# A graph layer on one core: the Relu moves from ScalarE to VectorE, and VectorE's register loads get new places

## The chip, the cores and the metric

The kernel runs on one core of one Trainium2 chip. The metric is device time in microseconds (us) of one execution, and lower is better. The engines are named as in the profile: PE is TensorE (PEld its weight loads), DVE is VectorE, ACT is ScalarE, POOL is GpSimd, SP is SyncE, which here only issues DMAs.

## What is computed

One message-passing layer over 12,500 nodes (48 numbers each) and 400,000 edges, sorted by their target `dst`, with 32 attributes per edge and 128 hidden numbers:

```
h = maximum(layernorm(x), 0)
for each edge e:  pre_e = [h[dst_e], h[src_e], attr_e] @ W1 + b1
                  hid_e = relu(pre_e)
                  msg_e = hid_e @ W2 + b2
out = x + segment_sum(msg, dst)
```

## The kernel before

The first stage (`node_tables`, about 95 us) multiplies the normalised nodes with the two node parts of W1. That leaves `tab_a` (for targets) and `tab_b` (for sources), tables in DRAM with one row of 128 numbers per node, and `bt`, the source table once more, transposed, in SBUF: one node is one column of 128 partitions.

The second stage (`windows`) takes the edges in tiles of 128 and in 391 chunks of 8 tiles. The loop over `c` is unrolled and its order is written by hand: what stands first in the program comes first in the queue of its engine. Three chunks are in work at once. For a chunk:

- **prepare** (chunk c): SP fetches 80 rows of `tab_a` (`rhs`), the edge attributes (`lhs`) and the targets (`row`). GpSimd fetches the source rows of most tiles from `tab_b` into `gb` (L402), one indirect DMA a tile. Each fetch is held back until a marked VectorE instruction some seven chunks earlier has run (`mark`, `paced`), so that the fetches are spread over a chunk. VectorE makes two one-hot patterns, `lhs` (L418) and `hot` (L424).
- **columns**: some tiles are not fetched. Their source rows are copied, one column at a time, from `bt` into a tile `gt` (L359), at an address held in a register. VectorE makes 75 columns a chunk in four parts (19, 20, 20, 16) and ScalarE 72 in five (16, 16, 16, 12, 12), as the table `PARTS` says. Ahead of each part a register load (`load`, L324) reads the addresses from SBUF into registers of that engine. In total 446 of the 3125 tiles are made so, at most two a chunk.
- **before, turned** (chunk c - 1): TensorE multiplies the one-hot `lhs` and the attributes with `rhs` into `pre` in PSUM (L436), and for the tiles made by columns it turns `gt` and adds it there (L445).
- **hidden** (chunk c - 1): VectorE adds `gb` to `pre` in place, for the fetched tiles (L460, 896 or 768 numbers per partition), and then ScalarE makes the Relu of all 1024 into `hid` (L463).
- **fold** (chunk c - 2): TensorE sums `hid` over edges of one target, `p_g` (L471), and counts edges (L476).
- **add** (chunk c - 2): VectorE adds `p_g` into a segment of 1024 nodes in SBUF at a register's place (L490).

Twelve chunks make a segment. At its end VectorE clears the next one and copies the overlap (`segment_next`, L506 and L508). In the next two chunks TensorE multiplies the finished one with W2 (`p_f`, L516 and L517), each half behind `turned`, and VectorE adds it to x (L518) ahead of its `hidden`.

VectorE's queue in one round of the loop before is: lhs, load 0, 19 copies, hot, load 1, 20 copies, load 2, 20 copies, (L518), pre add, load 3, segment add, 16 copies. ScalarE's is: copies of parts 4 to 6, Relu, copies of parts 7 and 8, with one of the loads one chunk ahead.

Of the kernel before, what the change touches and what calls it, by code (L numbers as in the profile page):

```python
# [8 lines left out]
F32 = mybir.dt.float32  # L9
I32 = mybir.dt.int32  # L10
AF = mybir.ActivationFunctionType
ALU = mybir.AluOpType
# [4 lines left out]
P = 128  # L17
N, D, DE, HID, E = 12500, 48, 32, 128, 400000
# [4 lines left out]
T = 8  # L23
CE = T * P
NCH = (NT + T - 1) // T
# [20 lines left out]
BF16 = mybir.dt.bfloat16  # L46
# [13 lines left out]
    (False, 75, 16, 76),  # L60
    (False, 91, 16, 92),
    (False, 107, 16, 108),
    (False, 123, 12, 124),
    (False, 135, 12, 136),
)
PART = sum(n for _, _, n, _ in PARTS)
BASE = 148
DVE_PARTS = sum(dve for dve, *_ in PARTS)
BEHIND = len(PARTS) - 2

BT0 = 16512
SEG0 = 130592
SEG_SIZE = 8 * L


SEG, NEXT, SEG2 = 152, 153, 154
PLACE0 = 155
WIDTH = 156
SLOTS = (NCH + 2 + P - 1) // P
MOST = 32  # L80

# [11 lines left out]
def turned_at(c):  # L93

    return ((), (T - 1,), (T // 2 - 1, T - 1))[len(TURNED.get(c, ()))]
# [16 lines left out]
def node_tables(nc, tc, keep, bt, x, ident, w1, b1, tab_a, tab_b, loads, most, check, rest):  # L112
# [6 lines left out]
    with ExitStack() as es:  # L119
# [3 lines left out]
        ps_n = es.enter_context(tc.tile_pool(name="ps_n", bufs=3, space=PSUM))  # L123
# [9 lines left out]
        xs = []  # L133
# [59 lines left out]
        def table(j, wt, tv, dve):  # L193

            r0, rb = slices[j]
            rows = wt.shape[0]
            t = tabs.tile([P, rb, HID], F32, name="tab")
            for g in range(0, rb // 2, 2):
                n = min(2, rb // 2 - g)
                p_n = ps_n.tile([P, 2, 2 * HID], F32, name="p_n")  # L200
                for q in range(n):
                    nc.tensor.matmul(  # L202
                        p_n[:, q, :], hts[j][:rows, g + q, :],
                        wt.rearrange("k a h -> k (a h)"), start=True, stop=True,
                    )
                to = t[:, 2 * g : 2 * (g + n), :].rearrange("p r h -> p (r h)")
                of = p_n[:, :n, :].rearrange("p q h -> p (q h)")
                if dve and g % 4:
                    nc.vector.tensor_copy(to, of)
                else:  # L210
                    nc.scalar.copy(to, of)  # L211
            nc.sync.dma_start(tv[:, r0 : r0 + rb, :], t)

        def turned(j):
# [3 lines left out]
            for g in range(0, rb // 2, 4):  # L218
                n = min(4, rb // 2 - g)
                for k in range(2):  # L220
# [12 lines left out]
                    else:  # L233
                        nc.scalar.copy(to, of)

        for i in range(ns + 3):
            if i < ns:
                centre(i)
            if 0 <= i - 1 < ns:
                scale(i - 1)  # L240
            if 0 <= i - 2 < ns:
                turn(i - 2)
            if i == ns + 1:
                most()
            if i == ns + 2:
                check()
            if 0 <= i - 3 < ns:
                table(i - 3, wb, tb_v, i >= ns)
        for j in range(ns):
            turned(j)  # L250
        for j in range(ns):
            table(j, wa, ta_v, True)
        rest()


def windows(nc, tc, gp, bt, ident, idx, x_t, tab_a, tab_b, dst, edge_t, w1, w2s, b2s, out_t):
# [3 lines left out]
    with ExitStack() as es:  # L260
# [49 lines left out]
        st = {}  # L310
# [55 lines left out]
        def mark(ins, us):  # L366
            marks.append((ins, us))
# [74 lines left out]
        def turned(c):  # L442

            for t, j in zip(turned_at(c), TURNED.get(c, ())):
                nc.tensor.matmul(st[c]["pre"][:, t, :], gts.pop(j), ident, start=False, stop=True)  # L445

        def hidden(c):
            s = st[c]
            n, pre = s["n"], s["pre"]
            two = len(turned_at(c)) == 2  # L450
            half = T // 2
            to = n - len(turned_at(c))

            def added(x):

                if not two:
                    return x[:, :to, :]
                return x.rearrange("p (b t) h -> p b t h", b=2)[:, :, : half - 1, :]

            mark(nc.vector.tensor_add(added(pre), added(pre), added(s["gb"])), 1.0)  # L460
            spans[c], marks[:] = list(marks), []
            h = wp.tile([P, T, HID], F32, name="hid")
            nc.scalar.activation(h[:, :n, :], pre[:, :n, :], AF.Relu)  # L463
            s["h"] = h

        def fold(c):
            s = st[c]
# [56 lines left out]
        with tc.manual_schedule():  # L524
            for c in range(NCH + 2):
                if c < NCH:
                    prepare(c)
                if c >= NCH:
                    load(c, 0)
                    columns(c, 0)  # L530
                for part in range(1, DVE_PARTS - 1):
                    load(c, part)
                    columns(c, part)
                if 0 <= c - 1 < NCH:
                    before(c - 1)
                if 0 <= c - 2 < NCH:
                    fold(c - 2)
                if 0 <= c - 1 < NCH:
                    turned(c - 1)

                g, k = group(c - 2)
                if k == GQ - 3 or c == NCH - 1:
                    segment_load(g)
                if g > 0 and k < L // BLK:
                    segment_sum(g - 1, k, BLK)
                if g > 0 and k == STORE:
                    segment_store(g - 1, L)
                columns(c, DVE_PARTS)
                for part in range(DVE_PARTS + 1, BEHIND):
                    load(c, part)  # L550
                    columns(c, part)
                if 0 <= c - 1 < NCH:
                    hidden(c - 1)
                if DVE_PARTS > 1:
                    load(c, DVE_PARTS - 1)
                for part in range(BEHIND, len(PARTS)):
                    load(c, part)
                    columns(c, part)
                load(c + 1, DVE_PARTS)
                if 0 <= c - 2 < NCH:  # L560
                    add(c - 2)
                    if k == GQ - 1:
                        segment_next(g)
                if DVE_PARTS > 1:
                    columns(c, DVE_PARTS - 1)
                if c == NCH + 1:
                    segment_sum(g, 0, END_L)
                    segment_store(g, END_L)

                if c < PIECES:  # L570
                    s = slice(c * PIECE, (c + 1) * PIECE)
                    nc.sync.dma_start(out_t[:, s], x_t[:, s])
# [126 lines left out]
def tile_gnn_preln(  # L699
# [60 lines left out]
    with tc.tile_pool(name="keep", bufs=1) as keep, tc.tile_pool(  # L760
# [3 lines left out]
        def loads():  # L764

            nc.sync.dma_start(dsts, dst_cols)
            nc.sync.dma_start(b0f, first_f.rearrange("(o c) -> o c", o=1).to_broadcast([P, NCH]))
            nc.sync.dma_start(far, places)
            nc.sync.dma_start(srci[:, :FIRST], src_cols[:, :FIRST])
            nc.sync.dma_start(last, src_last)  # L770
            nc.sync.dma_start(tab_a[NPAD:, :], zrow)

            nc.gpsimd.tensor_scalar_add(b0f, b0f, HALF)
            full = NT // T
            nc.gpsimd.tensor_tensor(
                rel[:, : full * T].rearrange("p (c t) -> p c t", t=T),
                dsts[:, : full * T].rearrange("p (c t) -> p c t", t=T),
                b0f[:, :full].unsqueeze(2).to_broadcast([P, full, T]), op=ALU.subtract,
            )
# [12 lines left out]

            spare = keep.tile([P, D], F32, name="spare")
            nc.gpsimd.indirect_dma_start(
                out=spare, out_offset=None, in_=x[:, :],
                in_offset=bass.IndirectOffsetOnAxis(ap=srci[:, :1], axis=0),
            )

            rows_of = edge_t.rearrange("d e -> (d e)").rearrange("(n h) -> n h", h=HID)
            for rows in (P, P - 1, P // 2):  # L800
                for k in range(3):
                    unused = keep.tile([P, HID], F32, name=f"unused{rows}_{k}")
                    nc.gpsimd.indirect_dma_start(
                        out=unused[:rows], out_offset=None, in_=rows_of,
                        in_offset=bass.IndirectOffsetOnAxis(ap=srci[:rows, :1], axis=0),
                    )

        def rest():

            nc.sync.dma_start(w2s, w2)  # L810
# [106 lines left out]
```

## Time and profile before

| | before |
|---|---|
| time, median of 3 runs | 3684.37 us (3682.39 to 3684.98) |
| the profiled execution | 3680.5 us, its span 3678.7 us |
| granted TensorE clock, mean | 0.766 |
| GB/s moved by DMA, mean | 95 |

The profile comes from one execution. A row of its groups gives line, engine, operation, what is written and read, shape and count, then the total busy time, the mean length of one in ns, and the engine's idle time just before them with what ended it. "issue" is idle time that ends with nothing that the profile shows: the engine's own sequencer had not yet sent the next instruction. A name such as DVEq means that sequencer. A record of VectorE reaches past the start of the next one, so busy time of a group can be less than count times mean.

### The profile page before, as it was taken

The numbers are of one execution on the slowest core, as the hardware profiler recorded it, in microseconds if no ns is written. First come the engines' busy times: TensorE is split into PE (matmuls) and PEld (weight loads), VectorE is DVE, ScalarE is ACT, GpSimd is POOL, SyncE is SP. The second block draws the span as 40 slices with busy tenths as digits, with TensorE's granted clock in tenths as the row PEclk, the third lists the DMA queues.
The fourth block names the chain that finished last, engine by engine and source line by source line (L and its number), as shares of the span: only waits on it lengthen the run. The fifth ranks groups of instructions, "written<-read, shape, count | busy, mean of one in ns | idle before, by whom it ended". The sixth has DMA issues, their size and how long they took to land.

```text
span 3678.7 us, 108360 instructions
## 1 busy us (share of the span) xinstructions
PE 2699.4 (73%) x17087; PEld 2431.6 (66%) x17087; DVE 3079.3 (84%) x30969; ACT 3154.1 (86%) x28402; POOL 2652.6 (72%) x2715
## 2 busy tenths in 40 slices
PE   8677777767777777777777777767777777777776
PEld 5566666667666666666666766766666666666665
DVE  5688888888888888888888888888888888888886
ACT  4698888888888888888889888888888888888886
POOL 6777777777777777777777777777777777777771
PEclk9677777787787787777777777787777778777777
DMA  5533333333333333333333333333333333333331
GB/s 195 164 94 95 93 88 91 95 87 95 92 94 89 91 88 98 92 94 89 91 91 93 94 94 90 88 95 88 96 92 91 90 91 88 99 91 94 91 93 39
DMA packets 190484, 349.56 MB, mean 95 GB/s; under 512 B 64786, under 2 KB 96932, under 8 KB 188484
## 3 DMA queue, kind: packets, MB, share of 16 engines
q0 software_dynamic: 86768, 176.28, 19.1%
q1 hardware_dynamic: 102736, 166.15, 15.0%
q14 instruction: 581, 4.76, 0.4%
q8 instruction: 139, 2.28, 0.3%
q10 hardware_dynamic: 260, 0.10, 0.0%
HBM read 322.79 MB, written 22.07 MB: 94 GB/s over the span
## 4 chain that ended last, share of the span: by engine, by line
DVE 70%; issue 14%; PE 5%; DVEq 3%; POOL 2%; DMA 2%; ACT 1%; POOLq 0%; ACTq 0%
DVE gt L359 44%; DVE pre L460 9%; DVE hot L424 7%; DVE lhs L418 6%; DVEq L324 3%; DVE seg L490 3%; POOL gb L402 2%; PE p_g L471 2%; DMA gb<-tab_b,srci 2%; PE p_f L516 1%; PE p_f L517 1%; DVE seg L506 1%; DVE xseg L518 1%; PE pre L436 1%; ACT hid L463 0%
## 5 line engine op out<-in xcount | busy, mean ns | idle before, releaser
L402 POOL DMA_INDIRECT gb<-tab_b,srci x2679 | 2617.9, 977 | 941.8 <-issue 493.3
L359 ACT COPY gt<-bt 128x1 f32 x27936 | 2746.5, 187 | 113.3 <-issue 69.7
L359 DVE COPY gt<-bt 128x1 f32 x29152 | 1915.4, 144 | 472.3 <-issue 426.3
L471 PE MATMUL p_g<-hot,hid 128*128 128x80 f32 x6250 | 1122.4, 354 | 937.8 <-ACT hid L463 927.9
L471 PEld LDWEIGHTS p_g<-hot,hid 128*128 128x128 f32 x6250 | 1050.6, 262 | 1013.2 <-ACT hid L463 1002.8
L436 PEld LDWEIGHTS pre<-rhs,lhs 112*128 112x128 f32 x6250 | 984.4, 247 | 85.2 <-issue 85.2
L436 PE MATMUL pre<-rhs,lhs 112*128 112x128 f32 x6250 | 1007.2, 330 | 18.2 <-DMA row<-in_dst 18.2
L463 ACT ACTIVATE hid<-pre 128x1024 f32<-128x1024 f32 x391 | 400.1, 1023 | 353.6 <-DVE pre L460 350.8
L460 DVE TENSOR_TENSOR pre<-pre,gb 128x896 f32<-128x896 f32 (+2 forms) x391 | 418.2, 1070 | 1.5
L424 DVE TENSOR_TENSOR hot<-wnum,rel 128x640 f32<-128x640 f32 x391 | 318.1, 813 | 0.0
L418 DVE TENSOR_SCALAR lhs<-row,bw 80x1024 f32<-80x1024 int16 x391 | 292.0, 747 | 10.4 <-DMA row<-in_dst 10.4
L445 PE MATMUL pre<-ident,gt 128*128 128x128 f32 x892 | 276.4, 418 | 0.3
L476 PEld LDWEIGHTS <-ones 128*128 128x128 bf16 x3125 | 247.9, 135 | 0.0
L476 PE MATMUL p_g<-hot,ones 128*128 128x80 bf16 x3125 | 247.5, 242 | 0.0
L445 PEld LDWEIGHTS pre<-ident,gt 128*128 128x128 f32 x892 | 196.7, 280 | 0.9 <-DVE gt L359 0.5
L490 DVE TENSOR_TENSOR seg<-seg,p_g 128x160 f32 x391 | 124.7, 319 | 13.3 <-DVE pre L460 5.2
L516 PE MATMUL p_f<-seg,w2s 128*48 128x512 f32 (+1 forms) x134 | 108.5, 906 | 0.4 <-DVE seg L490 0.4
L517 PE MATMUL p_f<-seg,b2s 1*48 1x512 f32 (+1 forms) x134 | 86.8, 733 | 0.0
L518 DVE TENSOR_TENSOR xseg<-xseg,p_f 48x512 f32<-48x512 f32 (+1 forms) x67 | 44.9, 670 | 47.4 <-PE p_f L517 47.4
L517 PEld LDWEIGHTS p_f<-seg,b2s 1*48 1x48 f32 x134 | 12.9, 141 | 89.4 <-issue 89.4
L506 DVE MEMSET seg<- 128x944 f32 x64 | 54.1, 845 | 9.5 <-issue 0.3
L211 ACT COPY tab<-p_n 128x512 f32<-128x512 f32 x33 | 18.7, 588 | 21.9 <-PE p_n L202 16.9
(66 smaller groups left out, 276.9 us busy)
## 6 DMA issues: line engine op xcount, KB each, us to landing
row<-in_dst SPq DMA_DIRECT2D x390, 160.0 KB
lhs<-in_edge_t SPq DMA_DIRECT2D x390, 128.0 KB
gb<-tab_b,srci POOLq DMA_INDIRECT x2679
rhs<-tab_a SPq DMA_DIRECT2D x391, 40.0 KB
xseg<-in_x_t SPq DMA_DIRECT2D x33, 192.0 KB
out_x<-xseg SPq DMA_DIRECT2D x33, 192.0 KB
tab_b<-tab SPq DMA_DIRECT2D x3, 1280.0 KB
tab_a<-tab SPq DMA_DIRECT2D x3, 1280.0 KB
```

The source lines that it names most:

```text
L359: done = copy(gts[of][:, e : e + 1], bt8[:, bass.ds(at, 4)].bitcast(F32))
L402: fetch = nc.gpsimd.indirect_dma_start(out=gb[:, t, :], out_offset=None, in_=tab_b[:, :], in_offset=bass.IndirectOffsetOnAxis(ap=srci[:, c ...
L418: mark(nc.vector.tensor_scalar(lhs[:W, : n * P], row[:, : n * P], bw[:, c : c + 1], None, op0=ALU.is_equal,), 0.8)
L424: mark(nc.vector.tensor_tensor(hot[:, :n, :], wnum.unsqueeze(1).to_broadcast([P, n, W]), rel[:, c * T : c * T + n].unsqueeze(2).to_broadca ...
L436: nc.tensor.matmul(pre[:, t, :], s["lhs"][:K, t * P : (t + 1) * P], s["rhs"][:K, :], start=True, stop=t not in turned_at(c),)
L445: nc.tensor.matmul(st[c]["pre"][:, t, :], gts.pop(j), ident, start=False, stop=True)
L460: mark(nc.vector.tensor_add(added(pre), added(pre), added(s["gb"])), 1.0)
L463: nc.scalar.activation(h[:, :n, :], pre[:, :n, :], AF.Relu)
L471: nc.tensor.matmul(p_g[:, 0, :], s["h"][:, t, :], s["hot"][:, t, :], start=t == 0, stop=t == n - 1)
L476: nc.tensor.matmul(p_g[:, 1, :], ones, high[:, t, 1::2], start=t == 0, stop=t == n - 1)
L490: mark(nc.vector.tensor_add(to, to, s["p_g"]), 0.25)
L516: nc.tensor.matmul(p_f[:, :n], w2s, seg[:, 0, s], start=True, stop=False)
```

## The change

`hidden` is split. `gathered` adds `pre` and `gb` on VectorE, but into `hid` in SBUF and not back into PSUM. `hidden` then takes the maximum with zero on VectorE, in place, on the fetched tiles, and a second VectorE instruction takes it from PSUM to `hid` for the one or two tiles made by columns. ScalarE has no Relu any more and only copies columns, in five parts of 16, 80 a chunk. With 155 columns a chunk, 389 * 155 // 128 = 471 tiles are made by columns.

VectorE's queue becomes: lhs, load 0, 19 copies, hot, load 1, 20 copies, (L518), gathered, load 2, 20 copies, hidden (one or two maxima), load 3, segment add, 16 copies. All of ScalarE's loads and copies stand at the end of the round. The new maximum is marked with 0.55 for the pacing of fetches.

Nine GpSimd fetches ahead of the tables whose results nobody reads are left out. A function `unused` is called behind the tables: some twenty small operations on VectorE, 24 on ScalarE and 32 on TensorE, whose results nobody reads.

```
 def hidden(c)  (before)
-            mark(nc.vector.tensor_add(added(pre), added(pre), added(s["gb"])), 1.0)
-            spans[c], marks[:] = list(marks), []
-            h = wp.tile([P, T, HID], F32, name="hid")
-            nc.scalar.activation(h[:, :n, :], pre[:, :n, :], AF.Relu)
-            s["h"] = h
+        def gathered(c):
+            s = st[c]
+            s["h"] = h = wp.tile([P, T, HID], F32, name="hid")
+            mark(nc.vector.tensor_add(apart(c, h, False), apart(c, s["pre"], False), apart(c, s["gb"], False)), 1.0)
+            spans[c], marks[:] = list(marks), []
+
+        def hidden(c):
+            s = st[c]
+            of = apart(c, s["h"], False)
+            mark(nc.vector.tensor_scalar(of, of, 0.0, None, op0=ALU.max), 0.55)
+            if turned_at(c):
+                nc.vector.tensor_scalar(
+                    apart(c, s["h"], True), apart(c, s["pre"], True), 0.0, None, op0=ALU.max
+                )
```

`apart(c, x, by_cols)` gives the tiles of x that were made by columns, or the others. The loop:

```
-                for part in range(1, DVE_PARTS - 1):
-                    load(c, part)
-                    columns(c, part)
+                load(c, 1)
+                columns(c, 1)
...
-                columns(c, DVE_PARTS)
-                for part in range(DVE_PARTS + 1, BEHIND):
-                    load(c, part)
-                    columns(c, part)
+                if 0 <= c - 1 < NCH:
+                    gathered(c - 1)
+                load(c, 2)
+                columns(c, 2)
                 if 0 <= c - 1 < NCH:
                     hidden(c - 1)
-                if DVE_PARTS > 1:
-                    load(c, DVE_PARTS - 1)
-                for part in range(BEHIND, len(PARTS)):
-                    load(c, part)
-                    columns(c, part)
-                load(c + 1, DVE_PARTS)
+                load(c, 3)
                 if 0 <= c - 2 < NCH:
                     add(c - 2)
                     if k == GQ - 1:
                         segment_next(g)
-                if DVE_PARTS > 1:
-                    columns(c, DVE_PARTS - 1)
+                columns(c, 3)
+                for part in range(DVE_PARTS, len(PARTS)):
+                    load(c, part)
+                    columns(c, part)
```

In `PARTS` the last two rows become `(False, 123, 16, 124)` and `(False, 139, 16, 140)`, and the places behind them in the table of numbers move by eight.

More of the change, by code (lines that the diff above doesn't have):

```diff
@@ L62 @@
     (False, 107, 16, 108),
-    (False, 123, 12, 124),
-    (False, 135, 12, 136),
+    (False, 123, 16, 124),
+    (False, 139, 16, 140),
 )
 PART = sum(n for _, _, n, _ in PARTS)
-BASE = 148
+BASE = 156
 DVE_PARTS = sum(dve for dve, *_ in PARTS)
-BEHIND = len(PARTS) - 2
 BT0 = 16512
-SEG0 = 130592
+SEG0 = 130720
 SEG_SIZE = 8 * L
-SEG, NEXT, SEG2 = 152, 153, 154
-PLACE0 = 155
-WIDTH = 156
+SEG, NEXT, SEG2 = 160, 161, 162
+PLACE0 = 163
+WIDTH = 164
 SLOTS = (NCH + 2 + P - 1) // P
@@ L234, in turned, with unused @@
                         nc.scalar.copy(to, of)
+        def unused():
+            bits = keep.tile([P, 2], I32, name="bits")
+            nc.vector.memset(bits[:, :1], 0)
+            nc.vector.memset(bits[:, 1:], -1)
+            ones16 = keep.tile([P, P], BF16, name="ones16")
+            nc.vector.tensor_copy(ones16, ident)
+            two = keep.tile([P, 16], I32, name="two")
+            of = xs[0].rearrange("p r d -> p (r d)")
+            bits_of = of.bitcast(I32)
+            for k in range(6):
+                nc.vector.tensor_scalar(
+                    two[:, 2 * k : 2 * k + 2], bits, bits_of[:, 5 * k : 5 * k + 1],
+                    bits_of[:, 200 - 7 * k : 201 - 7 * k], op0=ALU.bitwise_and, op1=ALU.bitwise_xor,
+                )
+            p_n = ps_n.tile([P, 2, 2 * HID], F32, name="p_n")
+            flat = p_n.rearrange("p a b -> p (a b)")
+            for k in range(6):
+                nc.vector.tensor_copy(flat[:, k : k + 1], of[:, 5 * k : 5 * k + 1])
+            one = keep.tile([P, 48], F32, name="one")
+            for k in range(8):
+                nc.scalar.copy(flat[:, 8 + k : 9 + k], of[:, 5 * k : 5 * k + 1])
+            for k in range(8):
+                nc.scalar.copy(one[:, k : k + 1], of[:, 5 * k : 5 * k + 1])
+            for k in range(8):
+                nc.scalar.copy(one[:, 16 + k : 17 + k], flat[:, 8 + k : 9 + k])
+            p_n = ps_n.tile([P, 2, 2 * HID], F32, name="p_n")
+            flat = p_n.rearrange("p a b -> p (a b)")
+            for k in range(8):
+                nc.tensor.matmul(flat[:, k : k + 1], ident, of[:, 5 * k : 5 * k + 1], start=True, stop=True)
+            for k in range(8):
+                nc.tensor.matmul(
+                    flat[:, 16 + 2 * k : 18 + 2 * k], ident, of[:, 5 * k : 5 * k + 58 : 57],
+                    start=True, stop=True,
+                )
+            halves = keep.tile([P, 384], BF16, name="halves")
+            nc.vector.tensor_copy(halves, of[:, :384])
+            for k in range(8):
+                nc.tensor.matmul(
+                    flat[:, 40 + 2 * k : 42 + 2 * k], ones16, halves[:, 5 * k : 5 * k + 58 : 57],
+                    start=True, stop=True,
+                )
+            p_n = ps_n.tile([P, 2, 2 * HID], F32, name="p_n")
+            flat = p_n.rearrange("p a b -> p (a b)")
+            for k in range(4):
+                nc.tensor.matmul(flat[:, k * P : (k + 1) * P], of[:, k : k + P], ident, start=True, stop=True)
+            for k in range(4):
+                nc.tensor.transpose(flat[:, k * P : (k + 1) * P], of[:, k : k + P], ident)
@@ L252, in node_tables @@
             table(j, wa, ta_v, True)
+        unused()
         rest()
@@ L445, in turned, with apart @@
                 nc.tensor.matmul(st[c]["pre"][:, t, :], gts.pop(j), ident, start=False, stop=True)
+        def apart(c, x, by_cols):
+            n = st[c]["n"]
+            if not turned_at(c):
+                return None if by_cols else x[:, :n, :]
+            if len(turned_at(c)) == 1:
+                return x[:, n - 1 : n, :] if by_cols else x[:, : n - 1, :]
+            x, last_of = x.rearrange("p (b t) h -> p b t h", b=2), T // 2 - 1
+            return x[:, :, last_of, :] if by_cols else x[:, :, :last_of, :]
+        def gathered(c):
[3 more added lines that the diff above has]
+            spans[c], marks[:] = list(marks), []
         def hidden(c):
             s = st[c]
[L449 to L460, printed above, removed]
-            spans[c], marks[:] = list(marks), []
-            h = wp.tile([P, T, HID], F32, name="hid")
-            nc.scalar.activation(h[:, :n, :], pre[:, :n, :], AF.Relu)
-            s["h"] = h
+            of = apart(c, s["h"], False)
+            mark(nc.vector.tensor_scalar(of, of, 0.0, None, op0=ALU.max), 0.55)
+            if turned_at(c):
+                nc.vector.tensor_scalar(
+                    apart(c, s["h"], True), apart(c, s["pre"], True), 0.0, None, op0=ALU.max
+                )
         def fold(c):
@@ L797, in loads @@
             )
[L799 to L806, printed above, removed]
         def rest():
```

## The prediction

> **What bounds the kernel now.** I read the page first, for the engines' shares and the chain that ended last.
>
> ```profile
> PE 2699.4 (73%) x17087; PEld 2431.6 (66%) x17087; DVE 3079.3 (84%) x30969; ACT 3154.1 (86%) x28402; POOL 2652.6 (72%) x2715
> ...
> DVE 70%; issue 14%; PE 5%; DVEq 3%; POOL 2%; DMA 2%; ACT 1%; POOLq 0%; ACTq 0%
> ```
>
> ScalarE (ACT) has the largest busy share, yet the chain gives it 1%; it gives VectorE (DVE) 70% and another 14% to "issue", time in which an engine has work in its program but nothing dispatched. So I went to the view of all waits, to see which way the two engines wait for each other.
>
> ```profile
> PE p_g L471 <- ACT hid L463: 927.9, 373, 7.2
> POOL gb L402 <- issue: 493.3, 1602, 1.9
> DVE gt L359 <- issue: 426.3, 818, 1.2
> ACT hid L463 <- DVE pre L460: 350.8, 364, 19.5
> POOL gb L402 <- DVE gt L359: 250.0, 668, 2.1
> ...
> DVE xseg L518 <- PE p_f L517: 47.4, 27, 8.5
> ```
>
> The columns are total us, times, longest. ScalarE waits for VectorE (350.8 us, at the Relu), TensorE waits for ScalarE, GpSimd (POOL) waits for VectorE's marks. VectorE waits for no engine except 47.4 us for the sums of a finished segment, and 426.3 us for its own register loads. VectorE's queue is the clock of the loop, and the time is its sum per chunk. The groups, by shape (total busy, mean ns of one, idle before):
>
> ```profile
> L359 ACT COPY gt<-bt 128x1 f32 x27936 | 2746.5, 187 | 113.3 <-issue 69.7 <-DMA gb<-tab_b,srci 5.8 <-ACT gt L359 1.6
> L402 POOL DMA_INDIRECT gb<-tab_b,srci x2679 | 2617.9, 977 | 941.8 <-issue 493.3 <-DVE gt L359 250.0 <-DVE seg L490 78.7
> L463 ACT ACTIVATE hid<-pre 128x1024 f32<-128x1024 f32 x390 | 399.4, 1024 | 344.5 <-DVE pre L460 341.7 <-PE pre L436 1.0 <-issue 0.2
> L460 DVE TENSOR_TENSOR pre<-pre,gb 128x896 f32<-128x896 f32 x332 | 361.7, 1090 | 1.5
> L424 DVE TENSOR_TENSOR hot<-wnum,rel 128x640 f32<-128x640 f32 x390 | 317.5, 814 | 0.0
> L418 DVE TENSOR_SCALAR lhs<-row,bw 80x1024 f32<-80x1024 int16 x390 | 291.4, 747 | 10.4 <-DMA row<-in_dst 10.4
> L490 DVE TENSOR_TENSOR seg<-seg,p_g 128x160 f32 x391 | 124.7, 319 | 13.3 <-DVE pre L460 5.2 <-PE p_g L476 3.4
> L460 DVE TENSOR_TENSOR pre<-pre,gb 128x768 f32<-128x768 f32 x57 | 54.5, 955 | 0.0
> L418 DVE TENSOR_SCALAR lhs<-row,bw 80x640 f32<-80x640 int16 x1 | 0.5, 536 | 0.0
> ```
>
> Then one chunk from close by: the chain inside 1832 to 1838 us (start, length, what), and the register loads (L324) in two windows there.
>
> ```profile
> 1831.97 0.55 DVE gt L359 x9
> 1832.51 0.80 issue
> 1833.31 1.12 DVE gt L359 x15
> 1834.44 0.06 DVEq L324
> 1834.50 0.12 DVE gt L359 x2
> 1834.62 1.00 DVE pre L460
> 1835.62 0.28 DVE seg L490
> ...
> 1836.87 0.66 DVE lhs L418
> 1837.53 0.21 issue
> ```
>
> ```profile
> L324 DVEq TENSOR_LOAD <-last x2: 1414/1414/1415, 1829.7 to 1831.8; - x2
> ```
>
> ```profile
> L324 DVEq TENSOR_LOAD <-last x1: 1151/1151/1151, 1834.3 to 1834.3; - x1
> ```
>
> A copy costs 0.55/9 = 0.061 us from start to start, while one is recorded at 0.144 (L359 on the page), so neighbours overlap by 0.08; I price every operation at its record less 0.08. A load of 20 numbers takes 1.41 us, one of 16 takes 1.15. The load is issued while earlier work is still queued: the one of 1831.8 starts with some nine copies left, hides behind them for 0.6 us, and VectorE then idles 0.80. The 16-number load that follows the pre add is issued at 1834.44, only 0.18 us ahead of that add, and is nearly covered by its 1.00 us. Behind lhs the idle is 0.21 us.
>
> Does the sum close? Per chunk 75 copies x 0.061 = 4.58; lhs 0.66, hot 0.73, pre 0.99, seg 0.24 = 2.62; idle 426.3/390 = 1.09, plus three lost overlaps of 0.08 = 1.33. That is 8.53, against a period of (3651.7 - 110.0)/390 = 9.08 from the row below, which gives the first and last start of lhs. The other 0.55 is the work at the end of each segment, which the change keeps (47.4/390 = 0.12 of it is the wait at L518), and what my sum misses.
>
> ```profile
> L418 DVE TENSOR_SCALAR lhs<-row,bw x391: 536/740/942, 110.0 to 3651.7; 80x1024 f32<-80x1024 int16 x195, 80x640 f32<-80x640 int16 x1
> ```
>
> **The change, part by part** (us per chunk on VectorE's queue).
>
> *The load that followed copies goes.* The chain a chunk earlier shows the idle behind hot:
>
> ```profile
> 1821.30 0.73 DVE hot L424
> 1822.03 0.13 issue
> ```
>
> Of 1.09 idle, 0.21 stand behind lhs and 0.13 behind hot, and those two places stay. The rest, 0.75 (0.80 in the chunk shown), plus the lost overlap 0.08, is **-0.83**.
>
> *The same 20 numbers now load behind the pre add* ("gathered"). This add waits for the same TensorE result and the same fetches as the add at L460, so I take the same 0.18 us of lead. The next copy would start 1.41 + 0.09 (from 1831.8 + 1.415 to 1833.31) - 0.18 = 1.32 after the add starts, where the add alone takes 1.00: 0.32 in this chunk, and 0.22 with a lead of 0.28. I take **+0.27**, between the two. Writing the sum to SBUF instead of PSUM: the segment add, PSUM and SBUF in and SBUF out, takes 0.319 for 160 elements; at the slope (1090 - 955)/128 = 1.055 ns per element that leaves 0.150 fixed, and the pre add leaves 0.145. No difference.
>
> *The maximum on the gathered tiles.* Tiles made by columns become 389 x 155 // 128 = 471 where 389 x 147 // 128 = 446 were, so 3125 - 471 = 2654 tiles stay, 6.79 a chunk, 869 elements. No row shows SBUF to SBUF float32 of this kind. The nearest is lhs, one tensor from SBUF to SBUF: (747 - 536)/384 = 0.549 ns per element, so 0.66 - 155 x 0.00055 = 0.58; without lhs's per-partition operand possibly 0.53. From the other side, at the add's 1.055 ns, 0.98. I take **+0.55**, as lhs has the same operation and memory, and keep 0.53 and 0.98.
>
> *The maximum on the turned tiles*, from PSUM: 471 x 128 / 391 = 154 elements, by the segment add of 160: **+0.24**.
>
> *The 16-number load behind the maxima*: 1.15 + 0.09 against 0.79 of maxima and whatever is queued ahead, between 0.18 (as at the pre add) and 0.55 (nine copies). The rest is 0.27 or nothing. The maximum waits for nothing from outside, so its lead is the longer one: **+0.03**.
>
> Sum: -0.83 + 0.27 + 0.55 + 0.24 + 0.03 = **+0.26 us**, over 390 chunks +101 us.
>
> *Segments.* In the second chunk of a segment VectorE stands before the sum of L518:
>
> ```profile
> 1807.02 1.02 ACT L463 ACTIVATE hid<-pre 128x1024 f32<-128x1024 f32 x1 [3.43 <-DVE pre L460]
> ...
> 1808.10 3.27 PE L471 MATMUL p_g<-hot,hid 128*128 128x80 f32 x16 [3.52 <-ACT hid L463]
> ...
> 1814.28 1.94 PE L517 MATMUL p_f<-seg,b2s 1*48 1x512 f32 x2
> ...
> 1816.25 0.68 DVE L518 TENSOR_TENSOR xseg<-xseg,p_f 48x512 f32<-48x512 f32 x1 [1.65 <-PE p_f L517]
> ```
>
> From hid to the end of p_f TensorE needs 1816.22 - 1808.04 = 8.2 us, and VectorE got there 1816.25 - 1.65 - 1808.04 = 6.6 after the Relu. After the change hid is ready behind the maximum, and VectorE then has the second maximum 0.24, seg 0.24, 16 copies 0.98, lhs with its stall 0.95, 19 copies 1.16, hot with its stall 0.95 and 20 copies 1.22 = 5.7 left. The wait grows by 0.9 in each of the 27 places that have it now, 24 us, and may begin in others: **+25 us**.
>
> *What costs nothing.* ScalarE loses the Relu and its wait and gains eight copies: 80 x 0.098 (2746.5/27936) = 7.9, and with 0.2 us of stall at each of five loads 8.9 at most, under the 9.3 of VectorE that covers it. GpSimd loses 25 fetches, and 6.79 x (0.977 + 0.30, the gap before a fetch in the row below) = 8.7 a chunk is still under VectorE. The unused GpSimd fetches that go ran while the tables were being built; the small operations that come stand where VectorE sits idle anyway until the first rows land (second row below).
>
> ```profile
> 1800.42 0.94 POOL L402 DMA_INDIRECT gb<-tab_b,srci  x1 [0.30 <-issue]
> ```
>
> ```profile
> 109.99 0.90 DVE L418 TENSOR_SCALAR lhs<-row,bw 80x1024 f32<-80x1024 int16 x1 [9.92 <-DMA row<-in_dst]
> ```
>
> Some twenty of them at 0.1 to 0.2 us fit into these 9.9 us; uncovered they would cost 4. The pre adds get shorter by 25 x 0.135 = 3.4 us. I set the two against each other.
>
> In all 101 + 25 = +126 on the profiled 3680.5 us (span 3678.7); the median of the runs is 3684.4, 3.9 above, and I add that: **3810 us**.
>
> **A rule that speaks against it.** The 0.55 stands on lhs, which runs beside GpSimd's fetches with a median of 740 ns and a maximum of 942, though GpSimd is busy 72% of the time. The Trainium skill, "SBUF — State Buffer", section "SBUF: two separate sides", says that a VectorE operation in a two-port mode and a GpSimd operation lock each other out for a whole instruction. By it a maximum that meets a fetch would wait half of 0.977, at 72% of the time: 0.35 us a chunk, +137 us. The narrow spread of lhs does not show such a block; it is kept as a rival.
>
> **Rivals.**
> *The maximum is slow* (one element per step, or held by a fetch): +0.35 to +0.43 more a chunk, 3945 to 3980 us. For it: no float32 row of the kind. Against: lhs. 0.08 for the first, 0.04 for the lock.
> *The load hides fully, and the kernel is faster.* If the load behind the pre add were issued with nine copies queued (0.55) and not 0.18, 1.41 + 0.09 - 0.55 is under 1.00 and the 0.27 goes; with the maximum at 0.53 and no wait for the last load the sum is -0.83 + 0.53 + 0.24 = -0.06, -23 us, and as hid is then early enough for the wait at L518 to grow by no more than 10 us, about 3671 us. It decides at a lead of 0.5 us. Against: the waits of the add stand where they stood, and held the lead to 0.18. 0.10.
> *ScalarE was the hidden brake*, so that freeing it gives its 350 us back: about 3450 us. Against: no VectorE row waits for ScalarE. 0.03.
> *The stall only moves*: the load behind the add keeps the 0.83 that it cost behind copies, +0.56 more, about 4030 us. Against: the 16-number load is covered there now. 0.05.
>
> **How the numbers follow.** The forecast has 0.70. Its own bounds: -0.83 + 0.22 + 0.53 + 0.22 = +0.14 with +10 of segments gives 3750; -0.83 + 0.32 + 0.60 + 0.25 + 0.15 = +0.49 with +25 gives 3900. The range runs to that upper end and reaches down to the faster rival at 3671, so it begins at 3670. It leaves out the slow maximum (0.12), the moved stall (0.05) and the brake (0.03), 0.20 together; the forecast's own range is 3750 to 3900. What a measurement can tell from no change is 0.2%, 7 us. Faster: 0.09 of the hidden load and 0.03 of the brake, 0.12. Within 0.2%: 0.01 of the hidden load and 0.04 from the low end of the forecast, 0.05. Slower: the rest, 0.83.
>
> **What would show it.** Right: DVE's issue idle before gt falls from 426 to about 300 us; the maximum's mean record is near 0.63 us and that of the turned tiles near 0.32; ACT idles more and waits on no pre; TensorE waits for DVE hid; xseg waits for p_f some 70 us; the lhs period is 9.4. Wrong: maxima near 1.0 us, a gt row that waits for something other than issue, a period below 9.08, or an ACT row that VectorE or TensorE waits for.

## The result, and the profile after

| | before | after |
|---|---|---|
| time, median of 4 runs | 3683.38 us (3681.42 to 3684.98) | 3721.44 us (3717.61 to 3724.93) |
| ratio, 95% interval | | 1.0103 (1.0086 to 1.0121) |
| span of the profiled execution | 3678.7 us | 3716.9 us |
| granted TensorE clock, mean | 0.766 | 0.750 |

The change makes the kernel 38 us slower. The forecast was slower by 126 us: the direction was right, the size three times too large. The time lies below the forecast's own range of 3750 to 3900, in the part that was added for the faster rival.

The page of the changed kernel, engines and chain:

```profile
PE 2778.1 (75%) x17189; PEld 2511.6 (68%) x17189; DVE 3361.6 (90%) x31788; ACT 3135.5 (84%) x31212; POOL 2671.2 (72%) x2681
...
DVE 73%; issue 7%; PE 6%; DVEq 4%; ACT 3%; DMA 2%; POOL 1%; ACTq 0%; SPq 0%; POOLq 0%
```

VectorE's busy time went from 3079.3 to 3361.6, +282.3 us. Its idle time went from 3678.7 - 3079.3 = 599.4 to 3716.9 - 3361.6 = 355.3, -244.1 us. What is left, 38.2, is the difference of the spans. It must be, as busy and idle add up to the span for every engine; that VectorE is the engine to look at follows from the waits below. Two large amounts nearly cancel, and the share of "issue" in the chain falls from 14% to 7%.

From all waits of the changed kernel (total us, times, longest):

```profile
PE p_g L528 <- DVE hid L517: 898.0, 377, 6.1
...
ACT gt L408 <- PE pre L494: 385.0, 157, 5.9
...
DVE gt L408 <- issue: 184.9, 730, 0.8
...
DVE xseg L575 <- PE p_f L574: 47.1, 33, 3.8
```

TensorE now waits for VectorE's maximum where it waited for ScalarE's Relu. ScalarE waits mostly for free `gt` tiles, that is, it runs ahead. In the loop VectorE still waits for hardly anything but its own loads and `p_f`. The groups (busy, mean ns, idle before), first VectorE's copies before, which the prediction had not shown, then the changed kernel's rows, and the first and last start of lhs:

```profile
L359 DVE COPY gt<-bt 128x1 f32 x29152 | 1915.4, 144 | 472.3 <-issue 426.3
```

```profile
L408 DVE COPY gt<-bt 128x1 f32 x29175 | 1917.0, 144 | 239.8 <-issue 184.9 <-ACT gt L408 3.8 <-DMA rhs<-tab_a 3.7
...
L517 DVE TENSOR_SCALAR hid<-hid 128x896 f32<-128x896 f32 x307 | 192.7, 628 | 0.0
...
L519 DVE TENSOR_SCALAR hid<-pre 128x128 f32<-128x128 f32 x307 | 86.6, 282 | 0.0
...
L517 DVE TENSOR_SCALAR hid<-hid 128x768 f32<-128x768 f32 x82 | 46.4, 565 | 0.0
...
L519 DVE TENSOR_SCALAR hid<-pre 128x256 f32<-128x256 f32 x82 | 34.1, 416 | 0.0
```

```profile
L467 DVE TENSOR_SCALAR lhs<-row,bw x391: 541/740/921, 106.0 to 3694.8; 80x1024 f32<-80x1024 int16 x195, 80x640 f32<-80x640 int16 x1
```

The period is (3694.8 - 106.0)/390 = 9.20 us, from 9.08. And one chunk of the chain (start, length, what), to be laid beside the one of before:

```profile
1834.66 0.73 DVE gt L408 x10
1835.39 0.01 issue
1835.40 0.38 DVE gt L408 x4
1835.78 0.06 DVEq L373
1835.84 0.12 DVE gt L408 x2
1835.96 1.00 DVE hid L510
1836.96 0.20 issue
1837.16 0.82 DVE gt L408 x12
```

The load of 20 numbers (DVEq L373) is issued 0.18 us ahead of the add, the add covers most of it, and 0.20 us of idle are left where 0.80 stood behind the copies.

### The profile page after: what moved, and what is told of

It is laid out like the page before. It is cut to its first block, busy times and chain, and to the rows that moved or that the text cites. A ratio compares the mean times of both kernels' runs of the same rounds, so it can differ in the third digit from the quotient of the medians.

```text
span 3716.9 us, 112385 instructions
## 1 busy us (share of the span) xinstructions
PE 2778.1 (75%) x17189; PEld 2511.6 (68%) x17189; DVE 3361.6 (90%) x31788; ACT 3135.5 (84%) x31212; POOL 2671.2 (72%) x2681
## 4 chain that ended last, share of the span: by engine, by line
DVE 73%; issue 7%; PE 6%; DVEq 4%; ACT 3%; DMA 2%; POOL 1%; ACTq 0%; SPq 0%; POOLq 0%
DVE gt L408 42%; DVE hid L510 9%; DVE hot L473 6%; DVE lhs L467 5%; DVE hid L517 5%; DVEq L373 4%; PE p_g L528 3%; ACT gt L408 3%; DMA gb<-tab_b,srci 2%; DVE seg L547 2%; DVE hid L519 2%; PE p_f L573 1%; POOL gb L451 1%; PE p_f L574 1%; DVE seg L563 1%
## 5 line engine op out<-in xcount | busy, mean ns | idle before, releaser
L408 ACT COPY gt<-bt 128x1 f32 x31113 | 3086.4, 187 | 494.8 <-PE pre L494 385.0
L451 POOL DMA_INDIRECT gb<-tab_b,srci x2654 | 2649.8, 998 | 965.5 <-issue 464.7
L408 DVE COPY gt<-bt 128x1 f32 x29175 | 1917.0, 144 | 239.8 <-issue 184.9
L528 PE MATMUL p_g<-hot,hid 128*128 128x80 f32 x6250 | 1141.5, 358 | 898.5 <-DVE hid L517 898.0
L485 PEld LDWEIGHTS pre<-rhs,lhs 112*128 112x128 f32 x6250 | 1010.1, 253 | 77.8 <-issue 77.7
L485 PE MATMUL pre<-rhs,lhs 112*128 112x128 f32 x6250 | 1029.0, 334 | 9.5 <-DVE lhs L467 9.5
L510 DVE TENSOR_TENSOR hid<-pre,gb 128x896 f32<-128x896 f32 (+2 forms) x391 | 411.7, 1053 | 0.6
L494 PE MATMUL pre<-ident,gt 128*128 128x128 f32 x942 | 301.6, 436 | 12.1 <-DVE gt L408 12.1
L517 DVE TENSOR_SCALAR hid<-hid 128x896 f32<-128x896 f32 (+2 forms) x391 | 240.2, 614 | 0.1
L494 PEld LDWEIGHTS pre<-ident,gt 128*128 128x128 f32 x942 | 218.8, 297 | 13.4 <-issue 10.4
L519 DVE TENSOR_SCALAR hid<-pre 128x128 f32<-128x128 f32 (+1 forms) x389 | 120.7, 310 | 0.0
L575 DVE TENSOR_TENSOR xseg<-xseg,p_f 48x512 f32<-48x512 f32 (+1 forms) x67 | 45.0, 672 | 47.2 <-PE p_f L574 47.1
```

What stands on the lines that cost most here:

```text
L408: done = copy(gts[of][:, e : e + 1], bt8[:, bass.ds(at, 4)].bitcast(F32))
L451: fetch = nc.gpsimd.indirect_dma_start(out=gb[:, t, :], out_offset=None, in_=tab_b[:, :], in_offset=bass.IndirectOffsetOnAxis(ap=srci[:, c ...
L485: nc.tensor.matmul(pre[:, t, :], s["lhs"][:K, t * P : (t + 1) * P], s["rhs"][:K, :], start=True, stop=t not in turned_at(c),)
L510: mark(nc.vector.tensor_add(apart(c, h, False), apart(c, s["pre"], False), apart(c, s["gb"], False)), 1.0)
L517: mark(nc.vector.tensor_scalar(of, of, 0.0, None, op0=ALU.max), 0.55)
L519: nc.vector.tensor_scalar(apart(c, s["h"], True), apart(c, s["pre"], True), 0.0, None, op0=ALU.max)
```

## The experiments

The theory on record was the sum of VectorE's queue: every operation costs its own length, and a register load costs what the queued work does not cover. The rivals are named in the expectations.

**The new order alone, Relu on ScalarE.**

```
-                for part in range(1, DVE_PARTS - 1):
-                    load(c, part)
-                    columns(c, part)
+                load(c, 1)
+                columns(c, 1)
...
                 if 0 <= c - 1 < NCH:
                     hidden(c - 1)
-                if DVE_PARTS > 1:
-                    load(c, DVE_PARTS - 1)
+                load(c, 2)
+                columns(c, 2)
+                load(c, 3)
```

> The kernel before, with its Relu on ScalarE, but the 20-number load and its copies moved behind the pre add. Theory (the time is the sum of VectorE's queue, and a load costs what the queued work does not cover): the stall behind copies goes, -0.89 us a chunk; the load behind the add costs 0.21; but the 16-number load now follows 20 copies and no maximum, and shows 1.12 + 0.09 - 0.55 = 0.65 of its length. In all -0.03, about 3672 us (3650 to 3695). Rival A (the new order removes a whole stall whatever follows): -0.68, about 3420 us.

Measured: 3666.7 us, ratio 0.9953 (0.9939 to 0.9966). Two rows of its groups, the columns as above:

```profile
L359 DVE COPY gt<-bt 128x1 f32 x29152 | 1915.9, 144 | 234.5 <-issue 188.5 <-DMA rhs<-tab_a 3.5
...
L490 DVE TENSOR_TENSOR seg<-seg,p_g 128x160 f32 x391 | 125.9, 322 | 217.4 <-DVE gt L359 198.8 <-issue 15.3 <-PE p_g L476 3.2
```

In front of the copies 472.3 - 234.5 = 238 us of idle went; in front of the segment add, which now stands behind the 16-number load, 217.4 - 13.3 = 204 came. The releaser that the row names, "DVE gt", had long been done. It is the load: at all 388 such places of the trace the segment add starts 0.09 us after the load's end. So the order by itself moves the stall to the next load and gains 16 us, near the theory's 12. Rival A falls.

**The Relu on VectorE alone**, order and columns of before:

```
+            s["h"] = h = wp.tile([P, T, HID], F32, name="hid")
+            mark(nc.vector.tensor_add(added(h), added(pre), added(s["gb"])), 1.0)
             spans[c], marks[:] = list(marks), []
-            h = wp.tile([P, T, HID], F32, name="hid")
-            nc.scalar.activation(h[:, :n, :], pre[:, :n, :], AF.Relu)
-            s["h"] = h
+            mark(nc.vector.tensor_scalar(added(h), added(h), 0.0, None, op0=ALU.max), 0.55)
...
+                nc.vector.tensor_scalar(halves[0], halves[1], 0.0, None, op0=ALU.max)
```

> The kernel before, with its order of loads and 72 columns on ScalarE, but the Relu taken as maxima on VectorE right behind the pre add. Theory: 0.53 for the maximum on fetched tiles, 0.26 for that on turned tiles, less 0.04 of the load's remainder that they now cover, some 0.1 more if the maximum waits for the add just ahead: +0.75 to +0.85 a chunk, 3975 to 4015 us. Rival B (ScalarE, freed of the Relu and of its wait, gives back what VectorE pays, and the new order is worth little): +40 to +60, about 3735 us.

Measured: 4153.1 us, ratio 1.1281 (1.1264 to 1.1298), 140 us above the theory's range and far from rival B. The queue in one chunk (start, length, operation, idle before):

```profile
1832.15 1.08 DVE L461 TENSOR_TENSOR hid<-pre,gb 128x896 f32<-128x896 f32 x1
1833.26 0.63 DVE L463 TENSOR_SCALAR hid<-hid 128x896 f32<-128x896 f32 x1
1833.80 0.28 DVE L469 TENSOR_SCALAR hid<-pre 128x128 f32<-128x128 f32 x1
1834.47 0.32 DVE L495 TENSOR_TENSOR seg<-seg,p_g 128x160 f32 x1 [0.38 <-issue]
```

The load of 16 numbers in this stretch:

```profile
L324 DVEq TENSOR_LOAD <-last x1: 1104/1104/1104, 1833.3 to 1833.3; - x1
```

The maximum starts when the add's record ends (1833.26 after 1832.15 + 1.08), with no overlap: it waits for the add's result. The load is behind it in the program, and it starts only when the maximum does: 0.02 us behind its start in this chunk, and likewise in the others. So it is held back as well, and of its 1.1 us the two maxima cover only their own length: 0.38 of idle before the segment add, 157.6 us in all. My expectation had let the maxima cover the load there. The theory's rule holds, my use of it did not: an operation that waits covers nothing that is issued behind it until it starts.

**The Relu on VectorE where it covers no load and waits for nothing**, behind the segment add:

```
+                if 0 <= c - 1 < NCH:
+                    maxima(c - 1)
                 if DVE_PARTS > 1:
                     columns(c, DVE_PARTS - 1)
```

`maxima` holds the two instructions; these lines follow the segment add.

> The kernel before, order and 72 columns kept, with both maxima on VectorE behind the segment add, where the load that the pre add already covers is over and the add's result has been waited for. Theory: the maxima cover no load and wait for nothing, so they cost their length, 0.53 + 0.24 = 0.77 a chunk, about 3985 us (3965 to 4010): between the 4153 of the maxima right behind the pre add, which held the next load back, and the 3721 of the changed kernel, where they cover one. Rival F (the 4153 us came from VectorE doing the Relu at all, by contention with GpSimd or with ScalarE's copies): about 4150 us again.

> As e7_relu_behind_add, once more. Where the kernel before takes 3683 us, theory: 3965 to 4010 us, a ratio near 1.082. Rival F (the Relu on VectorE costs as much wherever it stands): about 4150 us, 1.128.

The first of these ran on a chip on which the kernel before took 4453 us; more of that below. The second: 3940.1 us, ratio 1.0700 (1.0684 to 1.0717).

```profile
L359 DVE COPY gt<-bt 128x1 f32 x29152 | 1914.2, 144 | 456.7 <-issue 410.4 <-DMA rhs<-tab_a 3.7 <-ACT gt L359 1.7
...
L472 DVE TENSOR_SCALAR hid<-hid 128x896 f32<-128x896 f32 (+2 forms) x391 | 239.7, 613 | 0.2
```

+258 us is 0.66 a chunk, some 25 us below the range: the maxima cost their records less the overlaps (busy 3367.3 against 3079.3, +288), and the idle ahead of copies (-15.6) and of L518 (47.4 to 36.8) fell a little. Rival F falls: the same operations cost 258 us here and 470 right behind the add, and the two kernels differ in their place alone.

**The maximum left out of the changed kernel**, on the fetched tiles:

```
         def hidden(c):
             s = st[c]
-            of = apart(c, s["h"], False)
-            mark(nc.vector.tensor_scalar(of, of, 0.0, None, op0=ALU.max), 0.55)
```

> The changed kernel with the maximum on the fetched tiles left out (their numbers go on without the Relu, so the output is not the layer's). Theory: 0.53 us a chunk goes, but the 16-number load behind it then shows: 1.12 + 0.09 less some 0.45 of queued copies and 0.22 of the other maximum = 0.54, where 0.03 shows now. In all about -0.02, 3712 us (3690 to 3728). Rival E (the maximum costs its own length): -0.53, about 3515 us.

> As e5_no_big_max, once more. Where the kernel before takes 3683 us, theory: 3712 us (3690 to 3728), a ratio of 1.002 to 1.012, as the maximum covers the 16-number load. Rival E (the maximum costs its own length): about 3515 us, 0.954.

In this kernel the numbers of the fetched tiles go on without the Relu. The second of these runs measured 3671.7 us, ratio 0.9974 (0.9964 to 0.9984): 50 us below the changed kernel, nearer to the theory's 10 than to the rival's 206, but outside both.

```profile
L545 DVE TENSOR_TENSOR seg<-seg,p_g 128x160 f32 x391 | 125.9, 322 | 154.0 <-DVE hid L517 145.1 <-issue 6.2 <-PE p_g L531 2.7
...
L573 DVE TENSOR_TENSOR xseg<-xseg,p_f 48x512 f32<-48x512 f32 (+1 forms) x67 | 44.9, 671 | 29.3 <-PE p_f L572 29.0
```

VectorE's busy time falls from 3361.6 to 3188.8, 173 us; idle ahead of the segment add rises from 8.9 to 154.0, 145 us. So the maximum had covered 0.37 us a chunk of the last load. A further 18 us come off the wait at L518 (47.2 to 29.3), which the expectation lacked; hid is ready earlier without the maximum, which would explain it. And 9 us come off the idle ahead of copies.

**72 columns on ScalarE** in the changed kernel (the last two parts have 12, as before).

> The changed kernel with 72 columns a chunk on ScalarE instead of 80 (446 tiles by columns, 2679 fetches). Theory: VectorE's queue is the same but for 25 tiles that change from one maximum to the other and back into the add, so 3721 us within 8. Rival C (the eight more columns, by saving 25 fetches of 1.3 us on GpSimd, hid a part of the forecast loss): 3755 us or more.

Measured: 3721.5 us, ratio 1.0109 (1.0094 to 1.0124). The eight columns and 25 fetches make no difference that shows; rival C falls.

**The unused operations**, back as they were before.

> The changed kernel without the small unused operations behind the tables, and with the nine unused fetches of the kernel before back in their place. Theory: none of them stands in the loop; the first round started at 106.0 us in the changed kernel and at 110.0 before, so 3721 us with -4 to +5. Rival D (the unused operations made up some of the gap between forecast and result): 30 us or more either way.

> As e3_unused_as_before, once more, since on the chip of that call the kernel before itself took 4453 us. Theory: 3721 us with -4 to +5 where the kernel before takes 3683, a ratio of 1.009 to 1.012. Rival D (the unused operations made up some of the gap between forecast and result): a ratio 0.008 or more away from 1.010.

The second measured 3730.3 us, ratio 1.0138 (1.0123 to 1.0154): 9 us slower than the changed kernel, just out of the theory's range and short of rival D. lhs starts at the same place:

```profile
L466 DVE TENSOR_SCALAR lhs<-row,bw x391: 536/739/934, 105.8 to 3699.1; 80x1024 f32<-80x1024 int16 x195, 80x640 f32<-80x640 int16 x1
```

First start 105.8 against 106.0, last 3699.1 against 3694.8, and 26.2 against 22.1 us from there to the end of the span. So it isn't the stage where these operations stand (the profile of the changed kernel has 16 of them on VectorE). The profiled executions are 8.4 us apart, and 7.1 of these stand in the waits for `p_f`:

```profile
DVE xseg L574 <- PE p_f L573: 54.2, 36, 7.5
```

Half of that is the longest wait, at the end of the program, 7.5 us against 3.8. The kernel of the next experiment keeps the unused operations and has one of 7.6 there, so they do not decide it; why it is long in some kernels and short in others is open.

**Fewer columns on VectorE**, to use what the above says: the load behind the add gets 16 numbers, which 1.00 us covers.

```
-    (True, 39, 20, 40),
-    (True, 59, 16, 60),
+    (True, 39, 16, 40),
+    (True, 55, 16, 56),
```

> The changed kernel with 71 columns a chunk on VectorE instead of 75: the load behind the add has 16 numbers, not 20 (151 columns, 458 tiles). Theory: four copies less, -0.24, and the 16-number load behind the add shows 1.12 + 0.09 - 0.20 - 1.00 = 0.01 instead of 0.21: -0.44 a chunk, 3550 us by VectorE alone; GpSimd's 6.82 fetches a chunk at 1.30 make 8.87, which would hold it at about 3600. So 3550 to 3610. Rival (VectorE's queue is not what bounds the changed kernel): 3721 us or a little more, as there are 13 fetches more.

Measured: 3570.2 us, ratio 0.9700 (0.9685 to 0.9714), 3% under the kernel before. Groups, and GpSimd's waits:

```profile
L408 DVE COPY gt<-bt 128x1 f32 x27584 | 1818.2, 144 | 170.5 <-issue 118.3 <-ACT gt L408 5.4 <-DMA rhs<-tab_a 3.7
L510 DVE TENSOR_TENSOR hid<-pre,gb 128x896 f32<-128x896 f32 (+2 forms) x391 | 413.6, 1058 | 11.8 <-DMA gb<-tab_b,srci 5.5 <-issue 4.6 <-PE pre L485 0.7
```

```profile
POOL gb L451 <- issue: 285.3, 936, 0.3
POOL gb L451 <- DMA gb<-tab_b,srci: 259.1, 850, 0.3
POOL gb L451 <- DVE gt L408: 161.3, 529, 0.3
```

The copies take 98.8 us less and the idle ahead of them 69.3 less, together 168 where the spans differ by 149; other rows gave some back, the idle ahead of the add among them (0.6 to 11.8). Of the 69 us, 66 stood behind the add (78.3 to 12.1 us, summed over all chunks of both traces). So four copies fewer are worth more here than the smaller load. Once the loop runs, no wait of GpSimd is longer than 0.3 us: its fetches run back to back. But the add waits for them for 11.8 us at most in all, so they did not hold the time at 3600, and VectorE's queue is what is left.

**71 columns on VectorE, 84 on ScalarE.** First with ScalarE's parts as 17, 17, 17, 17, 16, then as 20, 16, 16, 16, 16.

> 71 columns a chunk on VectorE and 84 on ScalarE (four parts of 17, one of 16): 155 columns as in the changed kernel. With 71 and 80 GpSimd never waited longer than its usual gap, so its fetches, 1.31 us from start to start, set the time there; 13 fetches less make -17 us against 3570. Theory: about 3553 us (3540 to 3565), with VectorE just under it. Rival G (VectorE or ScalarE sets the time already, ScalarE with four more copies): 3570 us or more.

> 71 and 84 columns again, but in parts of 20, 16, 16, 16 and 16, so that each register load starts at a multiple of four numbers and reads a multiple of four; in e8_71_84 the loads of 17 that started at 89, 106 and 123 took 3.8 us each on ScalarE, the one at 72 took 1.29 and the one of 16 at 140 took 1.06. Theory: the loads of ScalarE take 1.0 to 1.4 us again, and GpSimd's 2654 fetches of 1.31 us set the time: 17 us under e6_71_columns, about 3553 us (3540 to 3565). Rival G (ScalarE's four more copies or VectorE set the time): 3570 us or more. Rival H (more than 80 copies a chunk are slow on ScalarE for another reason): far above 3600.

The first took 6794 us, ratio 1.5259 (1.5238 to 1.5280), on the chip where the kernel before took 4453. Three of ScalarE's loads in it, of 17 numbers from place 72, 17 from place 89, and 16 from place 140:

```profile
L373 ACTq TENSOR_LOAD <-last x1: 1268/1268/1268, 3001.4 to 3001.4; - x1
```

```profile
L373 ACTq TENSOR_LOAD <-last x1: 3712/3712/3712, 3003.8 to 3003.8; - x1
```

```profile
L373 ACTq TENSOR_LOAD <-last x1: 1033/1033/1033, 3016.9 to 3016.9; - x1
```

With parts of 20 and 16, on a usual chip, ScalarE's loads take 1.05 us (median), and the time is 3562.8 us, ratio 0.9663 (0.9646 to 0.9680): the fastest kernel here. Rival H falls. The time lies in the theory's range, but not for the theory's reason, so that is luck. The gain over 3570 is 7 us and not 17, and small beside the spread of this kernel's own executions (3551 to 3565). The fetches had not set the time there:

```profile
L510 DVE TENSOR_TENSOR hid<-pre,gb 128x896 f32<-128x896 f32 (+2 forms) x391 | 411.7, 1053 | 0.6
```

With 13 fetches less the add hardly waits at all (0.6 us against 11.8), and what is left is VectorE's own queue.

**The other chip.** The first runs of the three repeated kernels shared that chip: 4404.6 us without the unused operations (ratio 0.9889, 0.9874 to 0.9904), 4499.8 without the maximum (1.0096, 1.0077 to 1.0115), 4472.7 with the maxima behind the segment add (1.0047, 1.0032 to 1.0063). Copies have the usual 144 and 187 ns there, but in the first of them ScalarE idles for "issue" ahead of its copies for 643.8 us, where the changed kernel has 70.6, and VectorE for 676.5, where it has 184.9. I draw nothing on the change from these times, since the idle time that the change works on is another there; why that chip is so is not known.

## Why the prediction was wrong in size

What held: VectorE's queue sets the time. On the usual chips it waits in the loop for little but its own loads and `p_f`, less work on it made the kernel 151 us faster (71 columns), and less work on ScalarE gave nothing (72 columns). The maximum runs at lhs's pace, 0.614 - 0.08 = 0.53 us against 0.55 forecast. The rival by which a fetch would hold a maximum for half its length falls: the row of the maximum (shortest, median, longest ns) is narrow, and nine in ten of those on 896 numbers took at most 624 ns, 7 above their median:

```profile
L517 DVE TENSOR_SCALAR hid<-hid x391: 494/616/820, 118.5 to 3705.5; 128x896 f32<-128x896 f32 x152, 128x768 f32<-128x768 f32 x42, 128x1024 f32<-128x1024 f32 x1, 128x640 f32<-128x640 f32 x1
```

What the Trainium skill says in "SBUF — State Buffer", "SBUF: two separate sides", that a two-port VectorE operation and a GpSimd operation lock each other out for a whole instruction, does not show on the maximum. On GpSimd's side there is little: a fetch takes 998 ns on the mean after the change, 977 before, and 983 without the maximum. No run here shows whether the maximum is such an operation, or whether these 21 ns come from it.

What failed, in the terms of the sum, 126 forecast and 38 measured:

- **The segments, "+25 us": 0.** The waits at L518 are 47.4 us before and 47.1 after. The step counted on the same 27 waits, each 0.9 us longer. Two chunks of the changed kernel show what it left out (columns: us, busy of PE, PEld, DVE, ACT, POOL, PEclk, DMA share, GB/s):

```profile
1820.00:1826.00 6.00, 5.88 (x30) 3.38 (x30) 5.53 (x60) 5.71 (x59) 4.76 (x5) 0.72 0.19 49
2814.00:2822.00 8.00, 8.00 (x32) 5.01 (x31) 4.89 (x57) 3.54 (x36) 5.20 (x6) 0.50 0.19 51
```

```profile
1826.29 0.68 DVE L575 TENSOR_TENSOR xseg<-xseg,p_f 48x512 f32<-48x512 f32 x1 [0.43 <-PE p_f L574]
```

```profile
2822.62 0.68 DVE L575 TENSOR_TENSOR xseg<-xseg,p_f 48x512 f32<-48x512 f32 x1 [3.47 <-PE p_f L574]
```

  At a granted clock of 0.72 the wait is 0.43 us, at 0.50 it is 3.47. The chunk read for the prediction was at 0.54 (the same window of before, 1808 to 1816 us), and that was no rare one. For the second addition of each of the first 32 segments I took the clock of the 8 us ahead of it from the trace:

| granted clock | before: places, mean wait | after: places, mean wait |
|---|---|---|
| under 0.70 | 23, 1.41 us | 13, 2.26 us |
| 0.70 to 0.82 | 3, none | 9, 0.48 us |
| above 0.82 | 6, none | 10, none |

  At a low clock the mean wait grew by 0.85 us, close to the forecast's 0.9. But ten fewer places ran at a low clock, and the last three additions of the program waited 8.1 us where they had waited 13.6; the first additions of the segments went from 1.5 to 5.4 us. That the total stayed where it was is chance as far as these traces show; why fewer places ran at a low clock is open.
- **The loads, "-0.83" and "+0.27" and "+0.03": -207 us forecast, -232 measured** (472.3 - 239.8 ahead of the copies). I took the stall behind copies from the 426.3 us that the waits view names "issue", less 0.21 behind lhs and 0.13 behind hot. But that view counts 818 waits where three such stalls stand in each of 389 chunks: it leaves out short ones, and of the 389 behind hot it has only 61. Summed from the trace by what stands ahead, the idle ahead of copies was 323.8 us behind copies, 92.7 behind lhs and 55.6 behind hot. After the change it is 9.9, 97.5 and 53.7, and 78.3 behind the add. So the stall that went was 314/390 = 0.81 us and not 0.75, which makes 21 us. The load behind the add was well priced: 0.20 of idle and 0.08 of lost overlap against "+0.27". The "+0.03" behind the maxima, 12 us, did not show: the idle ahead of the segment add is 8.9 us, and was 13.3. The places behind lhs, hot and the add take some 7 us back.
- **The maxima, "+0.55" and "+0.24": 308 us forecast, about 293 measured** (busy +282.3, with 6.5 less in the adds and 4.6 less in lhs and the segment adds).
- The rest, some 23 us, is what the prediction had set against each other or at nothing: 11 us of those shorter adds and lhs, 6 us less idle before the first rows (10.4 to 4.7), 4 us less ahead of the segment add, and small rows.

So of the 88 us between 126 and 38 the loads, the segments and the rest make about 25 each, and the maxima 15. The way in which VectorE's queue adds up was right; the sizes of these terms, and for the segments the number of places, were not. The result is a difference of two amounts of 230 to 300 us, and errors of 5 to 11% in each, all to one side, count much in it. The forecast's range of its own should have been wider downwards.

One of the prediction's signs did not follow from its terms: 0.21 + 0.13 + 0.27 us of idle ahead of copies, less 0.08 of lost overlap, make 0.53 us a chunk, some 207 us in all, and not "about 300". Measured were 239.8 in the groups, 184.9 of it named "issue".

What the forecast did not say, and the runs show, is that the parts of the change are worth little or much by their places: the order alone -16 us, the Relu alone +470 or +258, both together +38. The maximum is 0.44 us a chunk of busy time in the changed kernel, and 0.37 of that it gives back by covering a load.

## What to carry to other kernels

On an engine whose queue sets the time, cost a register load by what is queued ahead of it, and put it behind a long operation that itself waits for nothing; a load behind a waiting operation is held with it. When two large terms cancel, take each from the whole idle and busy rows and not from one named releaser, and ask of a wait that depends on the clock how many places run at which clock. Taking work off VectorE did more than moving its loads: four copies less, and four numbers less behind the add, gave 4% against the changed kernel. Whether the same would pay with the Relu left on ScalarE was not run.

## What the hardware showed that I had not expected

A register load of 17 numbers took 3.71 us from place 89 and 1.27 from place 72, where 16 from place 140 took 1.03. In that trace the loads of 17 from places 89, 106 and 123 take 3.7 us in every chunk, and those from place 72 about 1.28. In the other kernels all loads of several numbers start at a multiple of four; those of 20 numbers took 1.41 on VectorE, and ScalarE's had a median of 1.04 on the same chip (the changed kernel without the unused operations). The slow loads were seen in one kernel and on one chip only. And one chip ran the kernel before in 4453 us and not 3683; the kernels traced there have copies of the usual length and longer gaps for "issue" between them.
